# First block of a two-block transformer kernel: queries and keys both scaled on VectorE, squares and scalings placed behind the values, beginning and end reordered

## The chip, the cores and the metric

The kernel runs on one core of a Trainium2 chip. A core has TensorE (PE in the profile; its weight loads are a row of their own, PEld), VectorE (DVE), ScalarE (ACT), GpSimd (POOL) and SyncE (SP), which here only issues DMAs. Each engine works off its own instructions strictly in the order in which they are written; engines wait for one another through semaphores. TensorE writes to PSUM, eight banks of 128 x 512 float32 numbers, and the other engines read the results from there. The metric is the device time of one execution in microseconds (us), lower is better; the median of three runs before the change is 2383.7 us (2383.65 to 2383.8).

## What is computed

All data are float32. The input x is 8 batches of 512 tokens of width 256. Two transformer blocks run one after the other. The change touches only the first; the second is left as it is. The first block, cut to what matters:

```python
mod = silu(c) @ adaln_w.T + adaln_b          # 9 rows of 256: shift, scale, gate for three stages
h = modulate(ln(x), shift_sa, scale_sa)
q = ln(_heads(h, 16)) * qn_w + qn_b          # 16 heads of 16; keys the same with kn_w, kn_b
k = ln(_heads(h, 16)) * kn_w + kn_b
v = _heads(h, 16)
x = x + gate_sa * softmax(q k / 4) v         # self-attention
h = modulate(ln(x), shift_ca, scale_ca)      # cross-attention with 64 context tokens
x = x + gate_ca * (softmax(q' k' / 4) v' @ ca_out_w.T + ca_out_b)
h = modulate(ln(x), shift_ff, scale_ff)
x = x + gate_ff * (silu(h @ w1.T) * (h @ w3.T) @ w2.T)
```

Queries, keys and values of the self-attention have no projection: the normalised heads of one batch are transposed once, and the transposed tile is scaled twice, into q and into k.

## The kernel before

**Stages in a pipeline over batches.** `fast_path` gives each batch three objects: `SelfAttention` (sa), `CrossAttention` (ca) and `FeedForward` (ff). `beginning()` runs the self-attention of batch 0 together with the set-up (modulation, keys and values of the context). Then `cycle(c)` for c = 1 to 7 runs the self-attention of batch c (s), the cross-attention of batch c-1 (x), the feed-forward of batch c-2 (up) and the second half of the feed-forward of batch c-3 (down), and prepares the self-attention of batch c+1 (nxt). In cycle 1 it also makes the second block's keys of the context (`keys1`). `ending()` finishes the last cross-attention and the last two feed-forwards and opens the second block. All of this is under a manual schedule for PE, DVE, ACT and POOL: the order of the calls is the order of the instructions on each of these engines. SP's order is left to the planner.

**Groups.** A batch's self-attention is four groups g = 0 to 3 (s0 to s3 below) of four heads. A group has four key tiles kt. `score(g, kt)` makes four products of 512 columns, one bank each, one for each head (they run side by side in four row strips of TensorE), and `exponentials` turns each into a tile p on ACT. `value(g, kt)` multiplies p with the values, which carry a column of ones for the sum of the softmax; all four kt add into one bank, which ACT copies to `oT` (L565). `back(g)` transposes it, divides and adds to x. `group` (L712) sets the order: the first two scores, then what is `beside`, the other two scores, what is `short`, the values, and the `rest`. In each cycle a further group of two scores and two values, the cross-attention's, stands between s2 and s3 (the "x group" below).

**Queries and keys.** `queries_keys(g)` (L534) transposes four tiles of z into one bank; ACT makes q of it (L543) and DVE makes k (L544). The next group's scores need both. z itself comes from four steps for each half c of the heads: `centre` (DVE, L512 to L514), `square` (ACT, L518), `var` (DVE, L524 and L525) and `scale` (POOL, a power of -1/2 at L531 and a product at L532).

**The ring of banks.** `bank()` and `bank_x()` deal the eight PSUM banks out in turn: the n-th request waits until the reader of request n-8 is done. So the order of the requests decides which reader a matmul waits for.

**The sums of the cross-attention.** `value(c)` of the cross-attention copies the sums to `den` and sends them through DRAM to be laid out anew; `inverse(c)` (L648) takes reciprocals and sends them through DRAM again to be spread over partitions as `rb`, of which there is one buffer; `scaled(c)` (L658, DVE) multiplies `oT` with `rb`. The second `rb` can be loaded only when `scaled(0)` has read the first. `out` (L662) needs both scaled halves.

**The beginning.** The modulation of all batches is a product with `sc32`, which a DVE copy inside `setup` (L740) fills, behind the variance of the second set of heads.

Of the kernel before, what the change touches and what calls it, by code (L numbers as in the profile page):

```python
# [12 lines left out]
AF = mybir.ActivationFunctionType  # L13
# [31 lines left out]
def fast_path(ctx: ExitStack, tc: tile.TileContext, a: dict, out: bass.AP):  # L45
# [237 lines left out]
    nc.vector.scalar_tensor_tensor(scT, scT, 1.0, cT, ALU.add, ALU.mult)  # L283
    nc.vector.tensor_scalar_mul(scT, scT, 0.5)
    nc.vector.tensor_copy(sc0, scT[:, :, 0:1].to_broadcast([P, 2, P]))
    awake(6)
    for k in range(2):
        mm(first_mod, sc0[:, k, :], adaw[:, k, 0 : 2 * D], k == 0, False)
# [168 lines left out]
    class SelfAttention:  # L457
# [76 lines left out]
        def queries_keys(self, g):  # L534

            c, par = divmod(g, 2)
            ps = bank()
            lo = par * HD0
            for t in range(NT):
                nc.tensor.transpose(ps[:, t * P : (t + 1) * P], zs[c][:, t, lo : lo + P], ident)  # L540
            q = wk.tile([P, N], F32, tag="q", name="q", bufs=1)
            k = wk.tile([P, N], F32, tag="k", name="k", bufs=1)
            nc.scalar.activation(q, ps, AF.Identity, bias=qk_cols[:, 1:2], scale=qk_cols[:, 0:1])  # L543
            nc.vector.tensor_scalar(k, ps, col("kw"), col("kb"), ALU.mult, ALU.add)  # L544
            self.s[g] = (q, k)

# [175 lines left out]
    def beginning():  # L722
# [14 lines left out]
        def head_of(s, c, par=None):  # L737
            return [lambda: s.centre(c, par), lambda: s.square(c, par), lambda: s.var(c, par), lambda: s.scale(c, par)]

        def setup():  # L740
            nc.vector.tensor_copy(sc32[:, :, 0:B], scT)
            modulation()

        def bk_columns():
            nc.vector.tensor_scalar(bk_even, col("bk"), col("parity")[:, 0:1], 1.0, ALU.mult, ALU.mult)

        def ones_next():
            nc.gpsimd.memset(hs[1][:, :, :, HD0 + 1 : 32], 0.0)
            nc.gpsimd.memset(hs[1][:, :, :, HD0 : HD0 + 1], 1.0)

        scores, values = of_self(s, 0)
        group(scores, [lambda: s.first_modulated(fm, 0, 1), *head_of(s, 0, 1), setup, lambda: s.first_modulated(fm, 1)],
              [], values, [modulation_columns, lambda: s.queries_keys(1), *head_of(s, 1)])
        scores, values = of_self(s, 1)
        group(scores, [modulation_end, lambda: context0(0), lambda: spread(s.s["gate"], 0, G_SA, D), lambda: context0(1),
                       bk_columns, ones_next],
              [], values, [lambda: s.queries_keys(2), lambda: s.back(0), lambda: nxt.norm(0), lambda: nxt.norm(1)])
        scores, values = of_self(s, 2)
        group(scores, [lambda: keys0(0), lambda: nxt.norm(2), lambda: nc.gpsimd.memset(vb0, 0.0), lambda: keys0(1)],
              [lambda: s.queries_keys(3), lambda: s.back(1), ctx_pieces[0]], values,  # L760
              [lambda: nxt.centre(0), lambda: nxt.square(0), ctx_pieces[1]])
        scores, values = of_self(s, 3)
        group(scores, [lambda: nxt.var(0), lambda: nxt.scale(0), lambda: values0(0), lambda: values0(1), ctx_pieces[2],
                       lambda: nc.vector.tensor_copy(c32[:, :, 0:B], cT)],
              [lambda: s.back(2), lambda: values0(2), lambda: values0(3), modulation1], values,
              [lambda: nxt.centre(1), lambda: context1(0), lambda: context1(1), modulation1_columns,
               lambda: nxt.square(1), lambda: nxt.queries_keys(0), lambda: nxt.var(1), lambda: nxt.scale(1)])

    def cycle(c):

        s, nxt, prev = sa[c], of(sa, c + 1), sa[c - 1]
        x, done = ca[c - 1], of(ca, c - 2)
        up, down = of(ff, c - 2), of(ff, c - 3)
        keys = [lambda p=p: keys1(p) for p in range(NPAIR)] if c == 1 else [lambda: None] * NPAIR
        store = store_keys1 if c == 1 else lambda g: None

        scores, values = of_self(s, 0)
        group(scores, [keys[0], keys[1], lambda: done.out(0), lambda: done.out(1), lambda: up.prepare(0), lambda: up.prepare(1),
                       lambda: down.down(0), lambda: up.prepare(2)],
              [lambda: s.queries_keys(1), lambda: prev.back(3), up.turn, lambda: nxt.norm(0), lambda: nxt.norm(1)], values)  # L780
        scores, values = of_self(s, 1)
        group(scores, [keys[2], lambda: store(0), lambda: down.down(1), lambda: x.prepare(0), lambda: x.prepare(1),
                       lambda: up.up(0), lambda: x.prepare(2), keys[3], lambda: up.up(1)],
              [lambda: s.queries_keys(2), lambda: s.back(0), x.turn, lambda: nxt.norm(2)], values)
        scores, values = of_self(s, 2)
        group(scores, [keys[4], lambda: store(1), lambda: up.up(2), lambda: up.up(3), lambda: x.queries(0), lambda: x.queries(1)],
              [lambda: s.queries_keys(3), lambda: s.back(1), lambda: nxt.centre(0), lambda: nxt.square(0)], values)
        group([lambda: x.score(0), lambda: x.score(1)],
              [keys[5], lambda: up.up(4), keys[6], lambda: up.up(5), lambda: s.back(2), lambda: nxt.var(0), lambda: nxt.scale(0),
               lambda: nxt.centre(1)], [], [lambda: x.value(0), lambda: x.value(1)])  # L790
        scores, values = of_self(s, 3)
        group(scores, [keys[7], lambda: store(2), lambda: up.up(6), lambda: x.inverse(0), lambda: x.inverse(1), lambda: up.up(7),
                       lambda: x.scaled(0)],
              [lambda: nxt.queries_keys(0), lambda: nxt.square(1), lambda: x.scaled(1), lambda: nxt.var(1), lambda: nxt.scale(1)],
              values)
        store(3)

    def ending():

        x, last, up = ca[B - 1], ff[B - 1], ff[B - 2]  # L800
        for fn in (lambda: ca[B - 2].out(0), lambda: ca[B - 2].out(1), lambda: sa[B - 1].back(3), lambda: up.prepare(0),
                   lambda: up.prepare(1), lambda: ff[B - 3].down(0), lambda: up.prepare(2), lambda: x.prepare(0),
                   lambda: x.prepare(1), up.turn, lambda: ff[B - 3].down(1), lambda: x.prepare(2), lambda: up.up(0),
                   x.turn, lambda: up.up(1), lambda: up.up(2), lambda: x.queries(0), lambda: x.queries(1), lambda: up.up(3)):
            fn()
        group([lambda: x.score(0), lambda: x.score(1)], [lambda: up.up(4), lambda: up.up(5)], [],
              [lambda: x.value(0), lambda: x.value(1)])
        for fn in (lambda: up.up(6), lambda: x.inverse(0), lambda: x.inverse(1), open_block1, lambda: up.up(7),
                   lambda: x.scaled(0), lambda: first_norm(0), lambda: first_norm(1), lambda: up.down(0), lambda: x.scaled(1),
                   lambda: x.out(0), lambda: x.out(1), lambda: last.prepare(0), lambda: last.prepare(1),  # L810
                   lambda: up.down(1), lambda: last.prepare(2), lambda: first_norm(2), first_turn, last.turn):
            fn()
        for f in range(8):
            last.up(f)
# [1474 lines left out]
```

## Time and profile before

| | us |
|---|---|
| runs, median of 3 | 2383.7 |
| the profiled execution | 2381.86 |
| its span, first to last instruction | 2379.9 |
| first block with its loads, until `last.up` starts | 842.8 |
| of it: until the first scores of cycle 1 | 96.1 |
| cycles 1, 2, 3, 4, 5, 6, 7 | 74.4, 92.2, 96.2, 97.9, 99.5, 96.2, 94.2 |
| `ending()` until `last.up` | 96.3 |
| from there to the end (last feed-forward, second block) | 1537.1 |

The profile is of one execution, which took 2381.86 us, 1.8 us less than the median of the runs; 2.0 us of it lie outside the span. The page lists busy time for each engine, the granted clock of TensorE in tenths of full speed (PEclk), the chain of work that ended last, and groups of instructions with the idle time before them. In timelines, each row has the start, the time until the last of its instructions ended, the engine, the line of the kernel, what is written and read, the shape, the number of instructions, and in brackets how long the engine sat idle and what released it. A float32 matmul shows as two instructions, so one score of four heads and one kt is x8.

### The profile page before, as it was taken

Reading aid. Unit: us, or ns where it says so; the run is one execution under the profiler, and the core shown is the slowest. Engines: PE = TensorE matmul, PEld = TensorE weight load, DVE = VectorE, ACT = ScalarE, POOL = GpSimd, SP = SyncE. Lnnn points to the kernel's source line nnn. Section 1 sums busy time; section 2 is a strip of 40 time slices with the busy share of each in tenths; the row PEclk is TensorE's granted clock in tenths of the full one; section 3 lists DMA queues with packets and bytes.
Section 4 is the critical chain, followed back from the end, with each engine's and each line's share of the span. In section 5 each row is a group of like instructions: output and inputs, shape, how many; then the busy total and the mean of one; then the engine's idle time right before and its main releaser. Section 6 shows DMA issues by size and latency. Waiting matters only on the chain.

```text
span 2379.9 us, 31143 instructions
## 1 busy us (share of the span) xinstructions
PE 2321.5 (98%) x12372; PEld 1183.2 (50%) x12372; DVE 990.6 (42%) x1879; ACT 883.8 (37%) x1341; POOL 919.5 (39%) x581
## 2 busy tenths in 40 slices
PE   8999999999999899999999999999999999999998
PEld 4434535445355453344434443434354566567666
DVE  3544544444433334434443444444434555432110
ACT  3565455545553213433333334342423221221221
POOL 3553333223221005545455545454544544432110
PEclk8889999999999999999999999999999999999999
DMA  5121000000000300000010001000014222211000
GB/s 186 37 72 37 18 12 16 14 10 18 11 3 12 96 0 10 20 20 19 19 24 15 27 12 28 10 28 11 28 41 122 64 65 74 75 59 37 18 23 19
DMA packets 83738, 83.98 MB, mean 35 GB/s; under 512 B 42128, under 2 KB 59264, under 8 KB 83584
## 3 DMA queue, kind: packets, MB, share of 16 engines
q1 hardware_dynamic: 82104, 78.73, 11.3%
q8 instruction: 100, 1.64, 0.3%
q0 software_dynamic: 576, 2.10, 0.2%
q10 hardware_dynamic: 904, 1.07, 0.2%
q14 instruction: 54, 0.44, 0.1%
HBM read 71.83 MB, written 10.04 MB: 34 GB/s over the span
## 4 chain that ended last, share of the span: by engine, by line
PE 89%; ACT 3%; DVE 3%; DMA 2%; issue 1%; POOL 0%; SPq 0%; ACTq 0%; DVEq 0%; POOLq 0%
PE ps_P L88 40%; PE ps_B L88 26%; PE ps_X L88 7%; PE ps_S L88 6%; PE ps_D L88 5%; PE ps_O L88 4%; ACT p L589 2%; DMA rb<-rec 1%; DVE k L544 1%; PE ps_B L401 1%; ACT q L543 1%; DMA den<-den 0%; PE ps_B L572 0%; PE ps_B L540 0%; DVE z L514 0%
## 5 line engine op out<-in xcount | busy, mean ns | idle before, releaser
L589 ACT ACTIVATE p<-ps_B 128x512 f32<-128x512 f32 x576 | 291.7, 623 | 172.2 <-PE ps_B L88 172.1
L1028 ACT ACTIVATE p<-ps_P 128x1024 f32<-128x1024 f32 x256 | 244.9, 1026 | 95.4 <-PE ps_P L88 95.4
L88 PE MATMUL ps_P<-q,k 32*128 32x512 f32 x2048 | 238.9, 600 | 0.5 <-DVE t L1007 0.5
L88 PE MATMUL ps_B<-hT,w 128*128 128x512 f32 x512 | 235.1, 614 | 0.0
L1037 POOL TENSOR_TENSOR sm<-sm,p 128x1024 f32<-128x1024 f32 x64 | 174.9, 2733 | 139.5 <-ACT p L1028 139.4
L88 PE MATMUL ps_P<-p,v 128*32 128x512 f32 x2048 | 226.4, 594 | 0.0
L996 ACT COPY v<-ps_P 128x1024 f32<-128x1024 f32 x32 | 32.4, 1012 | 375.6 <-PE ps_P L88 375.6
L154 POOL TENSOR_TENSOR rstd<-rstd,mhalf 128x4 f32<-128x4 f32 x49 | 52.0, 1061 | 298.7 <-DVE rstd L153 297.3
L88 PEld LDWEIGHTS ps_P<-q,k 32*128 32x128 f32 x2048 | 100.0, 184 | 133.3 <-issue 105.6
L88 PEld LDWEIGHTS ps_B<-hT,w 128*128 128x128 f32 x512 | 98.4, 196 | 131.3 <-issue 106.1
L1037 DVE TENSOR_TENSOR sm<-sm,p 128x1024 f32<-128x1024 f32 x64 | 98.3, 1537 | 150.6 <-ACT p L1028 150.6
L88 PE MATMUL ps_B<-q,k 16*128 16x512 f32 x1024 | 144.6, 629 | 11.1 <-DVE k L544 9.3
L88 PEld LDWEIGHTS ps_P<-p,v 128*32 128x32 f32 x2048 | 63.3, 110 | 158.3 <-issue 134.8
L1035 POOL TENSOR_TENSOR sm<-p 128x1024 f32<-128x1024 f32 x32 | 79.1, 2471 | 160.8 <-ACT p L1028 160.8
L583 POOL TENSOR_TENSOR attn<-attn,gate 128x256 f32<-128x256 f32 x32 | 23.3, 728 | 303.1 <-DVE attn L581 302.0
L531 POOL TENSOR_TENSOR var<-var,mhalf 128x32 f32<-128x32 f32 (+1 forms) x17 | 87.5, 5149 | 112.7 <-DVE var L525 66.7
L1006 DVE TENSOR_TENSOR t<-ps_P,rope_c 128x1024 f32<-128x1024 f32 x64 | 78.4, 1224 | 106.3 <-POOL q L1010 65.9
L88 PE MATMUL ps_B<-p,h 128*32 128x512 f32 x1024 | 120.4, 604 | 0.0
L88 PE MATMUL ps_P<-hT,w_sa_wq 128*128 128x512 f32 x256 | 118.3, 605 | 0.0
L88 PE MATMUL ps_B<-w,hid 128*128 128x256 f32 x512 | 115.4, 384 | 2.5 <-DVE hid L697 2.5
L1035 DVE TENSOR_TENSOR sm<-p 128x1024 f32<-128x1024 f32 x32 | 39.2, 1225 | 185.9 <-ACT p L1028 185.9
L88 PE MATMUL ps_P<-hT,w_sa_wk 128*128 128x512 f32 x256 | 115.1, 592 | 0.0
(257 smaller groups left out, 3684.4 us busy)
## 6 DMA issues: line engine op xcount, KB each, us to landing
rb<-rec SPq DMA_DIRECT2D x128, 128.0 KB
rb<-rec_d SPq DMA_DIRECT2D x124, 128.0 KB
rb<-rec SPq DMA_DIRECT2D x16, 256.0 KB
out_dram<-x SPq DMA_DIRECT2D x15, 256.0 KB
x<-in_x_dram SPq DMA_DIRECT2D x7, 512.0 KB
gate<-modd SPq DMA_DIRECT2D x24, 128.0 KB
k_d<-q POOLq DMA_DIRECT2D x4, 512.0 KB, 3.4
v_d<-v SPq DMA_DIRECT2D x4, 512.0 KB
```

Source lines behind the costliest of these rows:

```text
L88: nc.tensor.matmul(o, lhsT, rhs, start=start, stop=stop)
L154: nc.gpsimd.tensor_tensor(r[:, :n], r[:, :n], mhalf[:, :n], ALU.pow)
L401: nc.tensor.transpose(ps[:, t * P : (t + 1) * P], z[:, t, k * P : (k + 1) * P], ident)
L531: nc.gpsimd.tensor_tensor(var, var, half, ALU.pow)
L543: nc.scalar.activation(q, ps, AF.Identity, bias=qk_cols[:, 1:2], scale=qk_cols[:, 0:1])
L544: nc.vector.tensor_scalar(k, ps, col("kw"), col("kb"), ALU.mult, ALU.add)
L589: nc.scalar.activation(p[i], ps, AF.Exp, scale=HD0 ** -0.5)
L996: nc.scalar.copy(s["v", half][:, t0 : t0 + 2, :], ps)
L1006: nc.vector.tensor_tensor(c, ps, rope_c[:, None, :].to_broadcast([P, 2, N]), ALU.mult)
L1028: nc.scalar.activation(pr, pss[u], AF.Exp, scale=HD1 ** -0.5)
L1035: eng.tensor_tensor(s["sm", g, u], s["p", g, 0, u], s["p", g, 1, u], ALU.add)
L1037: eng.tensor_tensor(s["sm", g, u], s["sm", g, u], s["p", g, kt, u], ALU.add)
```

## The change

- `sc32` is filled right after `scT` is made (L286), no longer inside `setup`.
- q is made by DVE as k is, from the same bank, with scale and bias as two operands (L543).
- `beginning()`: in group 0 the modulation stands between the square and the variance of the second set of heads; the other half of the heads, `queries_keys(1)`, the modulation's columns, its end and `context0(0)` follow the values. From group 1 on `queries_keys(g+1)` and `back(g-1)` stand ahead of the values. Keys and values of the context, the context's norm and the second block's modulation are dealt out anew; the first square of the next batch moves from group 2 to the front of group 3, its `centre(1)` and `queries_keys(0)` ahead of group 3's values.
- `cycle(c)`: the next batch's `square(0)` moves from the short part of s2, ahead of the values' copy on ACT, into the x group behind its scores; `square(1)` moves from the short part of s3 to beside it; `x.scaled(0)` and `x.scaled(1)` move back, the first to the end of the short part of s3, the second behind s3's values. In cycle 2 alone, `up.turn` moves from s0's short part to beside s1.
- `ending()`: `down(0)` and the preparation of the last cross-attention come first, `out` of the cross-attention before it later, `up.up` of six of its eight parts later relative to the scores, the last feed-forward's preparation ahead of `up.down(0)`, and `last.turn` ahead of `first_turn`.

```diff
+    nc.vector.tensor_copy(sc32[:, :, 0:B], scT)
...
-            nc.scalar.activation(q, ps, AF.Identity, bias=qk_cols[:, 1:2], scale=qk_cols[:, 0:1])
+            nc.vector.tensor_scalar(q, ps, qk_cols[:, 0:1], qk_cols[:, 1:2], ALU.mult, ALU.add)
...
         scores, values = of_self(s, 0)
-        group(scores, [lambda: s.first_modulated(fm, 0, 1), *head_of(s, 0, 1), setup, lambda: s.first_modulated(fm, 1)],
-              [], values, [modulation_columns, lambda: s.queries_keys(1), *head_of(s, 1)])
+        group(scores, [lambda: s.first_modulated(fm, 0, 1), *head_of(s, 0, 1)[:2], modulation, *head_of(s, 0, 1)[2:]],
+              [], values, [lambda: s.first_modulated(fm, 1), *head_of(s, 1)[:2], lambda: s.queries_keys(1), *head_of(s, 1)[2:],
+                           modulation_columns, modulation_end, lambda: context0(0)])
         scores, values = of_self(s, 1)
-        group(scores, [modulation_end, lambda: context0(0), lambda: spread(s.s["gate"], 0, G_SA, D), lambda: context0(1),
-                       bk_columns, ones_next],
-              [], values, [lambda: s.queries_keys(2), lambda: s.back(0), lambda: nxt.norm(0), lambda: nxt.norm(1)])
+        group(scores, [lambda: spread(s.s["gate"], 0, G_SA, D), lambda: context0(1), bk_columns, ones_next],
+              [lambda: s.queries_keys(2), lambda: s.back(0), lambda: nxt.norm(0), lambda: nxt.norm(1)], values,
+              [lambda: keys0(0)])
         scores, values = of_self(s, 2)
-        group(scores, [lambda: keys0(0), lambda: nxt.norm(2), lambda: nc.gpsimd.memset(vb0, 0.0), lambda: keys0(1)],
-              [lambda: s.queries_keys(3), lambda: s.back(1), ctx_pieces[0]], values,
-              [lambda: nxt.centre(0), lambda: nxt.square(0), ctx_pieces[1]])
+        group(scores, [lambda: nxt.norm(2), lambda: nc.gpsimd.memset(vb0, 0.0), lambda: keys0(1), ctx_pieces[0]],
+              [lambda: s.queries_keys(3), lambda: s.back(1), lambda: nxt.centre(0)], values,
+              [lambda: values0(0), lambda: values0(1)])
         scores, values = of_self(s, 3)
-        group(scores, [lambda: nxt.var(0), lambda: nxt.scale(0), lambda: values0(0), lambda: values0(1), ctx_pieces[2],
-                       lambda: nc.vector.tensor_copy(c32[:, :, 0:B], cT)],
-              [lambda: s.back(2), lambda: values0(2), lambda: values0(3), modulation1], values,
-              [lambda: nxt.centre(1), lambda: context1(0), lambda: context1(1), modulation1_columns,
-               lambda: nxt.square(1), lambda: nxt.queries_keys(0), lambda: nxt.var(1), lambda: nxt.scale(1)])
+        group(scores, [lambda: nxt.square(0), lambda: nxt.var(0), lambda: nxt.scale(0), lambda: values0(2), ctx_pieces[1],
+                       ctx_pieces[2], lambda: nc.vector.tensor_copy(c32[:, :, 0:B], cT)],
+              [lambda: s.back(2), lambda: values0(3), lambda: nxt.centre(1), lambda: nxt.queries_keys(0)],
+              [modulation1, *values],
+              [lambda: context1(0), lambda: nxt.square(1), lambda: context1(1), modulation1_columns,
+               lambda: nxt.var(1), lambda: nxt.scale(1)])
...
+        early, late = ([], [up.turn]) if c == 2 else ([up.turn], [])
...
-              [lambda: s.queries_keys(3), lambda: s.back(1), lambda: nxt.centre(0), lambda: nxt.square(0)], values)
+              [lambda: s.queries_keys(3), lambda: s.back(1), lambda: nxt.centre(0)], values)
         group([lambda: x.score(0), lambda: x.score(1)],
-              [keys[5], lambda: up.up(4), keys[6], lambda: up.up(5), lambda: s.back(2), lambda: nxt.var(0), lambda: nxt.scale(0),
-               lambda: nxt.centre(1)], [], [lambda: x.value(0), lambda: x.value(1)])
+              [keys[5], lambda: nxt.square(0), lambda: up.up(4), keys[6], lambda: up.up(5), lambda: s.back(2), lambda: nxt.var(0),
+               lambda: nxt.scale(0), lambda: nxt.centre(1)], [], [lambda: x.value(0), lambda: x.value(1)])
         scores, values = of_self(s, 3)
-        group(scores, [keys[7], lambda: store(2), lambda: up.up(6), lambda: x.inverse(0), lambda: x.inverse(1), lambda: up.up(7),
-                       lambda: x.scaled(0)],
-              [lambda: nxt.queries_keys(0), lambda: nxt.square(1), lambda: x.scaled(1), lambda: nxt.var(1), lambda: nxt.scale(1)],
-              values)
+        group(scores, [keys[7], lambda: store(2), lambda: up.up(6), lambda: x.inverse(0), lambda: x.inverse(1), lambda: nxt.square(1),
+                       lambda: up.up(7)],
+              [lambda: nxt.queries_keys(0), lambda: nxt.var(1), lambda: nxt.scale(1), lambda: x.scaled(0)],
+              values, [lambda: x.scaled(1)])
```

The new order of `ending()` (its three lists are written anew):

```python
for fn in (lambda: sa[B - 1].back(3), lambda: ff[B - 3].down(0), lambda: x.prepare(0), lambda: x.prepare(1),
           lambda: ca[B - 2].out(0), lambda: x.prepare(2), lambda: ca[B - 2].out(1), lambda: up.prepare(0),
           lambda: up.prepare(1), lambda: ff[B - 3].down(1), lambda: up.prepare(2), x.turn, up.turn,
           lambda: x.queries(0), lambda: x.queries(1), lambda: up.up(0), lambda: up.up(1)):
    fn()
group([lambda: x.score(0), lambda: x.score(1)], [lambda: up.up(2), lambda: up.up(3)], [],
      [lambda: x.value(0), lambda: x.value(1)])
for fn in (lambda: up.up(4), lambda: x.inverse(0), lambda: x.inverse(1), open_block1, lambda: up.up(5), lambda: up.up(6),
           lambda: x.scaled(0), lambda: up.up(7), lambda: x.scaled(1), lambda: x.out(0), lambda: x.out(1),
           lambda: last.prepare(0), lambda: last.prepare(1), lambda: up.down(0), lambda: last.prepare(2),
           lambda: first_norm(0), lambda: first_norm(1), lambda: up.down(1), lambda: first_norm(2), last.turn, first_turn):
    fn()
```

## The prediction

> **What bounds the kernel now.** I read the page first, then the run in stages, then TensorE's own timeline in the stages that show gaps.
>
> ```profile
> PE 2321.5 (98%) x12372; PEld 1183.2 (50%) x12372; DVE 990.6 (42%) x1879; ACT 883.8 (37%) x1341; POOL 919.5 (39%) x581
> ...
> PEclk8889999999999999999999999999999999999999
> ```
>
> TensorE is busy nearly all the time and no other engine is half busy, so time is gained only where TensorE idles or runs at a lower granted clock. Both occur early: the clock row is at 8 in the first slices.
>
> ```profile
> 19.94:40.91 20.97, 14.90 (x89) 4.55 (x88) 5.20 (x16) 9.81 (x19) 3.52 (x2) 0.76 0.81 276
> 40.91:60.45 19.54, 17.02 (x84) 6.34 (x84) 5.47 (x12) 9.82 (x19) 7.46 (x4) 0.83 0.01 2
> ...
> 262.59:358.77 96.18, 93.34 (x505) 46.88 (x505) 44.62 (x119) 51.47 (x99) 29.65 (x19) 1.00 0.06 14
> 358.77:456.65 97.88, 95.04 (x505) 47.47 (x505) 42.92 (x107) 51.56 (x99) 29.60 (x19) 0.98 0.05 14
> ...
> 746.46:842.79 96.33, 82.99 (x316) 52.71 (x317) 40.34 (x100) 16.84 (x28) 8.56 (x8) 0.94 0.20 61
> ```
>
> These are stages: length, then busy time of PE, PEld, DVE, ACT, POOL, then the clock. The second block, 1537 us after 842.79, is full and untouched. The first block has its holes in the beginning (19.94 to 96.06), in the ending (746.46 to 842.79), and once in each cycle. The beginning's first hole:
>
> ```profile
> 19.94 2.00 PE L88 MATMUL ps_B<-q,k 16*128 16x512 f32 x16
> 26.30 3.64 PE L88 MATMUL ps_B<-adaw,sc 128*32 128x512 f32 x16 [4.36 <-DVE sc L741]
> 29.87 3.80 PE L88 MATMUL ps_B<-q,k 16*128 16x512 f32 x16
> ```
>
> TensorE waits 4.36 us for a DVE copy of 0.17 us (L741) that stands behind a variance, and then runs at half rate: 3.80 us for scores that took 2.00. The hole of a cycle, in cycle 4 and, below it, the same place in cycle 7, where there is no next batch:
>
> ```profile
> 421.53 2.26 PE L88 MATMUL ps_B<-q,kb 32*128 32x512 f32 x14
> 425.95 1.12 PE L88 MATMUL ps_B<-q,kb 32*128 32x512 f32 x2 [2.16 <-ACT oT L565]
> 427.01 5.40 PE L88 MATMUL ps_B<-hT,w 128*128 128x512 f32 x8
> ```
>
> ```profile
> 715.09 2.19 PE L88 MATMUL ps_B<-q,kb 32*128 32x512 f32 x16
> 717.21 4.99 PE L88 MATMUL ps_B<-hT,w 128*128 128x512 f32 x11
> ```
>
> The eighth score needs the bank of `oT`; ACT copies it only after a square (L518, at 424.80) that waits for DVE's `centre`. Cycle 7 has no such square: there the feed-forward starts 2.12 us after the first score, in cycle 4 5.48 us after.
>
> **The beginning.** Worked through group by group with before's durations. The weights of the modulation are there: SP's next use of that load's semaphore was released by 13.85.
> - Group 0 (scores at 19.94). The modulation follows at 21.94, 16 matmuls in column strips, 1.72 us instead of 3.64. Scores 2 and 3 follow the exponentials out of the banks until 26. ACT: eight exponentials to 25.1, a square to 25.4, eight more (4.03) to 29.45; values end 30.4. Behind them transposes, modulation end and `context0(0)` fill TensorE until 34.1, while DVE makes q and k (0.8 each) by 32.5. Next scores 34.1, before 40.91.
> - Group 1: exponentials 35.3 to 43.3, values end 44, `keys0(0)` 1.7; next scores 45.7, before 60.45. The chain transposes, q on ACT, k on DVE stood behind the values there (57.16 to 60.45) and now lies beside the exponentials; context products at half rate (5.52 for eight) become 3.4.
> - Group 2: eight exponentials from 46.9, the copy of `keys0(1)`, eight more to 55.7, values 56.5, `values0` twice 1.7; next scores 58.2, before 75.34.
> - Group 3 loses some back. ACT reaches `square(0)` after eight exponentials at 63.4; var to 65.0; POOL power 5.4 and product 1.1 to 71.5. Now TensorE's transposes for cycle 1 stand ahead of group 3's values and wait for that; POOL's power for the context's norm (1.0) stands behind too, so DVE's context rows (1.3) and `c32` come at 74.1, and `modulation1` (1.1), values (3.5) and context transposes (1.3) end at 80.0. TensorE idles some 8 of 11 us here, so I add 2.4 for half rate: first scores of cycle 1 at 82.4, before 96.06. **13.7 us less**, bounds 9 (half rate also in group 2, and a longer group 3) and 17.
>
> **q on DVE.** DVE waited 118.8 us in all for ACT's q before k (29 of 32 waits). DVE takes 0.81 for k, so q is bounded by 0.81 (k's row) and 0.78 (ACT's row). [...] q and k are now ready 1.7 us after the transposes, beside 3.6 us of values; without that cover they would cost 1.6 a group. TensorE's waits for k before scores go: two of 0.28 in cycles 1 and 3 to 7, one in cycle 2: 13 x 0.28, **3.6 us less**. The wait of 0.62 at the start of cycles 3 to 7 is counted below.
>
> **The square behind the scores.** 5.48 minus 2.12 is 3.36; group times (306.28 to 343.92 against 696.01 to 730.36) give 3.29. Cycles 1 to 6: **19.8 us less**. The square then delays only the tanh of `up(4)`, whose banks are free of need for 3 us; POOL still has `scale(0)` ready some 6 us before its transposes.
>
> **The scalings behind the values give back.** In cycle 4, with X = 436.20, the start of the cross-attention's values:
>
> ```profile
> 453.12 0.69 DVE L660 TENSOR_TENSOR oT<-oT,rb 128x512 f32<-128x512 f32 x1 [2.41 <-DMA rb<-rec]
> 455.78 0.81 DVE L544 TENSOR_SCALAR k<-ps_B,cols 128x512 f32<-128x512 f32 x1 [1.97 <-ACT q L543]
> 457.63 0.69 DVE L660 TENSOR_TENSOR oT<-oT,rb 128x512 f32<-128x512 f32 x1 [1.04 <-DMA rb<-rec]
> ```
>
> `rb` has one buffer: the second load starts when `scaled(0)` is done (453.81) and lands 3.8 us later. After the change q, k and the variance stand ahead of `scaled(0)`: it starts at X+18.55 instead of X+16.9, `scaled(1)` ends at X+23.8 instead of X+22.1. TensorE, without its 0.62 wait, reaches the second half of `out(0)` at X+22.3: a stall of 1.5. `out` ends at X+27.1 instead of X+26.1, so **1.0 us more** at five passages (cycles 2 to 6), 5.0. Bounds: 0 (load lands faster) and 2 each. From cycle 1 to 2 the round trip through DRAM bounds already (`out` at 174.33), so the 1.6 us that k waited there bring nothing. Leaving cycle 7, `out` comes 7 us later and is covered. What SP has queued behind the waiting load are gates of the next cycle, needed 6 us on.
>
> **The clock.** After the hole of the x group the feed-forward ran at half rate in cycles 1, 2, 4, 5: 8.83 for sixteen in cycle 4 against 7.13 in cycle 7, 1.7; 1.7 for cycles 1 and 2; cycle 5 is 3.3 longer than cycle 3. Together 8.4. [...] By the row all 8.4 go; as cycle 7 also fell to half rate later, at 732, I take 70%, 5.9, and charge the five new stalls a third of 1.7 each, 2.8: **3.1 less**, bounds -4 and +8.
>
> **Cycle 2's `up.turn`.** Before it waited 2.3 us for z at 184.97; now its hT stands on ACT behind eight exponentials (4.03), ahead of `up(0)`: a stall of 3.1 for a saved 2.3 and its half rate. **0**, bounds ±2.
>
> **The ending**, from 746.46. Down, `out` twice and down again (17.3) cover the preparations; `up.turn` waits some 2 us for z, which shares one buffer with `x.turn`. The scores come at 779, the values at 788 instead of 798.17, but behind them stand 13.8 us of `up` where 13.9 stood before, while the second `rb` needs 24.9 from the start of the values (823.02 minus 798.17): `out` stalls 8.4 in one piece, before 2.6+0.5+4.4. Gained is the 3.3 us wait for z at 838.77 and 2.0 at 760.88, for a new 2 at `first_turn`. `last.up` starts 88.3 after, plus 4 for half rate: 92.3 instead of 96.33. **4.0 less**, bounds 0 and 8.
>
> **Sum.** 13.7 + 3.6 + 19.8 - 5.0 + 3.1 + 0 + 4.0 = 39.2. The profiled execution, 2381.86, becomes 2342.7; the runs lie 1.8 above it: 2344.
>
> **Rivals.**
> - The cycles give most back: each new `out` stall brings half rate (1.7 each) and the x group's half rate stays. Then 5.9 are not saved and the half rate costs 8.5 instead of 2.8, 11.6 in all: 2356. For it: cycle 7's fall at 732 without a hole of 2 us. Against: cycles 3 and 6 kept clock 1.00.
> - The beginning gives 5 and the ending nothing, because POOL's chain in group 3 and the DRAM trip bound: 2344+8.7+4 = 2357. For it: POOL's 5.4 us powers; against: groups 0 to 2 hold 17 us of serial waits.
> - No new stall at `out` and no half rate: 5.0+2.8+2.5 better: 2334.
> - Slower: the stall at `out` takes TensorE to half rate and holds it. Its place is the start of cycles 3 to 7; after the long wait at 172 fourteen `out` matmuls took 5.53 (sixteen took 3.72 at 458.58), about 2 us lost, the worst row there is. It decides from 9 us a passage (39.2/5 + 1.0), some 16 us of half rate at each; at 10 us the time is 2389. No row comes near it.
> - The change does not do what it says: the four engines keep the written order, only SP's DMAs are placed by the planner; `rb` or weight loads placed worse in the ending cost a few us, within the bounds.
>
> **Chances.** Forecast 0.60 (its own range 2335 to 2353), cycles giving back 0.14, beginning and ending weak 0.10, better 0.11, slower 0.05. The range 2331 to 2361 takes in all but the slower case and tails. A difference under 0.2% (4.8 us) can't be told from none: faster 0.93, same 0.02, slower 0.05.
>
> **What would show it.** Group 0's modulation matmul should start near 22 with no wait on `sc`; cycle 1's first scores near 82; in the x group no wait on `oT` and 2.1 us from first score to feed-forward; no DVE wait of k on ACT; a new wait of `out` on L660 of about 1.5 in cycles 3 to 7 and of 8 in the ending. Wrong: cycle times still 96 to 99, or `out` stalls over 5 us.

## The result, and the profile after

The kernel after the change takes 2347.12 us in the median of 4 runs (2343.39 to 2350.16); the kernel before took 2383.75 in the same comparison. The ratio is 0.9844 (95% interval 0.9824 to 0.9863). The profiled execution took 2344.22 us, its span is 2342.4.

The page of the kernel after, engine totals and clock row:

```profile
PE 2299.6 (98%) x12372; PEld 1174.4 (50%) x12372; DVE 1016.1 (43%) x1911; ACT 863.8 (37%) x1309; POOL 921.5 (39%) x581
...
PEclk9999999999999999999999999999999999999999
```

32 instructions have gone over from ACT to DVE, and the 8s at the start of the clock row have gone. The same kernel by stages (length, busy time of PE, PEld, DVE, ACT, POOL, clock, DMA share, GB/s):

```profile
19.70:34.05 14.35, 14.35 (x98) 5.25 (x97) 8.47 (x22) 9.36 (x19) 4.70 (x3) 1.00 1.07 361
...
238.84:333.60 94.76, 93.55 (x506) 46.78 (x505) 48.12 (x123) 49.29 (x94) 30.03 (x20) 0.98 0.05 14
333.60:428.84 95.24, 93.61 (x505) 46.79 (x505) 45.73 (x111) 49.29 (x94) 29.97 (x20) 0.98 0.05 14
...
709.96:803.96 94.00, 82.07 (x316) 52.66 (x317) 42.19 (x100) 16.24 (x28) 8.65 (x8) 0.93 0.21 63
```

Group 0 of the beginning is full: 14.35 us of 14.35, where before it was 14.90 of 20.97. Cycle 3, once 96.18, takes 94.76, and cycle 4, once 97.88, takes 95.24. But both granted clocks are now 0.98; cycle 3 had 1.00 before. The places that were holes, in TensorE's timeline of the kernel after:

```profile
21.63 1.92 PE L88 MATMUL ps_B<-adaw,sc 128*32 128x512 f32 x16
...
397.79 2.00 PE L88 MATMUL ps_B<-q,kb 32*128 32x512 f32 x16
399.72 7.13 PE L88 MATMUL ps_B<-hT,w 128*128 128x512 f32 x16
```

The modulation's matmul starts at 21.63 with no bracket behind it, so it waits for nothing. In the x group the feed-forward starts 1.93 us after the first score, where it took 5.48, and runs at full rate. What is new is a wait at the start of a cycle, here in all engines' timeline, cycle 5 (its first scores are at 428.84):

```profile
427.50 0.68 DVE L661 TENSOR_TENSOR oT<-oT,rb 128x512 f32<-128x512 f32 x1
...
430.77 0.70 PE L88 MATMUL ps_B<-w_o,oT 128*128 128x256 f32 x2
431.92 0.69 DVE L661 TENSOR_TENSOR oT<-oT,rb 128x512 f32<-128x512 f32 x1 [3.74 <-DMA rb<-rec]
432.67 3.29 PE L88 MATMUL ps_B<-w_o,oT 128*128 128x256 f32 x14 [1.20 <-DVE oT L661]
```

`scaled(0)` is done at 428.18, the second `rb` lands 3.74 us later, and TensorE, which has the first two matmuls of `out` behind it, idles for 1.20 us. In the ending of the kernel after it is the same wait, larger:

```profile
775.06 0.70 PE L88 MATMUL ps_B<-w_o,oT 128*128 128x256 f32 x2 [3.73 <-DVE oT L661]
780.46 6.28 PE L88 MATMUL ps_B<-w_o,oT 128*128 128x256 f32 x14 [4.70 <-DVE oT L661]
```

The two waits sum to 8.43 us, and the fourteen matmuls behind them take 6.28 against 3.29 above, at half rate (the clock record of this trace has half rate from 776.3 to 786.5).

Where the time went, stage by stage. `both` and `again` are runs described below: two parts of the change alone, and the kernel after a second time, on one chip. `best_d` is the fastest variant. Each column is one profiled execution.

| us | before | after | both | again | best_d |
|---|---|---|---|---|---|
| until the first scores of cycle 1 | 96.06 | 84.06 | 92.57 | 83.92 | 81.22 |
| cycles 1 and 2 | 166.53 | 154.78 | 154.85 | 154.70 | 154.50 |
| cycles 3 to 6 | 389.72 | 377.92 | 366.80 | 377.67 | 368.17 |
| cycle 7 | 94.14 | 93.20 | 93.40 | 93.10 | 91.76 |
| ending, until `last.up` | 96.34 | 94.00 | 95.39 | 92.35 | 86.51 |
| the rest, untouched | 1537.13 | 1538.47 | 1538.76 | 1536.69 | 1538.61 |
| end | 2379.92 | 2342.43 | 2341.77 | 2338.43 | 2320.77 |

Of the 37.5 us between before and after, 12.0 come from the beginning, 11.75 from cycles 1 and 2, 12.7 from cycles 3 to 7 and 2.3 from the ending; the untouched rest took 1.3 more.

### The profile page after: what moved, and what is told of

Read it like the earlier page. It is cut to its first block, busy times and chain, and to the rows that moved or that the text cites. A ratio compares the mean times of both kernels' runs of the same rounds, so it can differ in the third digit from the quotient of the medians.

```text
span 2342.4 us, 31156 instructions
## 1 busy us (share of the span) xinstructions
PE 2299.6 (98%) x12372; PEld 1174.4 (50%) x12372; DVE 1016.1 (43%) x1911; ACT 863.8 (37%) x1309; POOL 921.5 (39%) x581
## 4 chain that ended last, share of the span: by engine, by line
PE 93%; DVE 3%; DMA 2%; POOL 1%; ACT 1%; issue 1%; SPq 0%; ACTq 0%; POOLq 0%; DVEq 0%
PE ps_P L88 40%; PE ps_B L88 28%; PE ps_X L88 7%; PE ps_S L88 6%; PE ps_D L88 5%; PE ps_O L88 4%; DMA rb<-rec 2%; PE ps_B L541 1%; PE ps_B L402 1%; DMA den<-den 1%; PE ps_B L573 1%; DVE oT L661 0%; POOL var L532 0%; PE ps_X L402 0%; ACT p L590 0%
## 5 line engine op out<-in xcount | busy, mean ns | idle before, releaser
L584 POOL TENSOR_TENSOR attn<-attn,gate 128x256 f32<-128x256 f32 x32 | 23.5, 734 | 240.0 <-DVE attn L582 239.0
L88 PE MATMUL ps_P<-w_sa_wv,hT 128*128 128x512 f32 x256 | 114.9, 592 | 0.0
```

Source lines behind the costliest of these rows:

```text
L88: nc.tensor.matmul(o, lhsT, rhs, start=start, stop=stop)
L584: nc.gpsimd.tensor_tensor(attn, attn, gate.to_broadcast([P, NT, 4, HD0]), ALU.mult)
```

## Experiments

Each ratio is to the kernel before on the same chip. The runs were made on three chips, on which the kernel before had medians of 2382.5, 2384.5 and 2385.0, so a difference in us between runs of different chips carries up to 2.5 us of that.

| run | what it is | median us (range) | ratio, 95% interval |
|---|---|---|---|
| `before_q` | before, q on DVE | 2352.7 (2349.39 to 2354.68) | 0.9861 (0.9846 to 0.9877) |
| `before_square` | before, `square(0)` moved | 2356.75 (2354.71 to 2363.61) | 0.989 (0.9872 to 0.9908) |
| `before_both` | before with these two | 2346.03 (2343.56 to 2350.15) | 0.9842 (0.9828 to 0.9856) |
| `after_again` | after | 2343.57 (2340.23 to 2345.66) | 0.9829 (0.9816 to 0.9843) |
| `q_on_act` | after, q back on ACT | 2367.96 (2366.01 to 2373.77) | 0.9942 (0.992 to 0.9965) |
| `square_back` | after, `square(0)` back | 2353.19 (2340.59 to 2356.66) | 0.9856 (0.9824 to 0.9887) |
| `scaled_early` | after, scalings forward again | 2332.77 (2329.08 to 2339.46) | 0.9794 (0.9772 to 0.9816) |
| `rb_two` | after, two `rb` buffers | 2335.57 (2327.47 to 2336.66) | 0.9799 (0.9782 to 0.9816) |
| `old_beginning` | after with before's `beginning()` | 2346.13 (2345.69 to 2349.84) | 0.9844 (0.9829 to 0.9859) |
| `old_ending` | after with before's `ending()` | 2348.03 (2346.87 to 2349.04) | 0.9845 (0.983 to 0.986) |
| `best_b` | `rb_two` and two more edits | 2326.4 (2323.43 to 2332.59) | 0.9759 (0.9744 to 0.9774) |
| `best_d` | `best_b`, `up.turn` early | 2321.33 (2314.98 to 2326.53) | 0.9728 (0.9707 to 0.9748) |

**Undoing one part: q.** The first question was whether the cycles' gain hangs on the square alone, as the prediction had it.

```diff
-            nc.vector.tensor_scalar(q, ps, qk_cols[:, 0:1], qk_cols[:, 1:2], ALU.mult, ALU.add)
+            nc.scalar.activation(q, ps, AF.Identity, bias=qk_cols[:, 1:2], scale=qk_cols[:, 0:1])
```

> The changed kernel with q made by ACT again (L544), all else as changed. Theory (k's wait on ACT's q is what the move to DVE took away; hidden work otherwise): scores of the next group wait 0.28 again in most groups of cycles 1 to 7, and in the beginning q stands on ACT behind eight exponentials, so that group 1's and 3's scores come 1 to 2 us later: 4 to 7 us more than the changed kernel's 2347.1, so 2351 to 2354. Rival (the order alone made the gain, q's engine is hidden): no change, 2347, with DVE's waits for ACT's q back but no wait of TensorE.

It took 20.8 us more than the kernel after, so both expectations missed, the rival's by most. Its timeline at the start of cycle 5, all engines:

```profile
436.49 0.81 DVE L545 TENSOR_SCALAR k<-ps_B,cols 128x512 f32<-128x512 f32 x1 [5.07 <-ACT q L544]
...
437.35 2.00 PE L88 MATMUL ps_B<-q,k 16*128 16x512 f32 x16 [0.45 <-DVE k L545]
...
442.55 0.69 DVE L661 TENSOR_TENSOR oT<-oT,rb 128x512 f32<-128x512 f32 x1 [3.85 <-DMA rb<-rec]
443.30 2.93 PE L88 MATMUL ps_B<-w_o,oT 128*128 128x256 f32 x6 [3.32 <-DVE oT L661]
```

With q on ACT, k is late, `scaled(0)` behind it too, and the second `rb` lands after a cycle's start by 5.2 us instead of 3.1: `out` waits 3.32 us instead of 1.20. Cycles 3 to 6 take 99.0 to 99.7 us. Together they are 19.4 us longer than in the kernel after: 7.6 of it are waits of `out` and 1.8 waits for k, and up to 8.5 is half rate, of which they have 27.3 us instead of 10.2.

**Undoing one part: the square.**

```diff
-              [lambda: s.queries_keys(3), lambda: s.back(1), lambda: nxt.centre(0)], values)
+              [lambda: s.queries_keys(3), lambda: s.back(1), lambda: nxt.centre(0), lambda: nxt.square(0)], values)
...
-              [keys[5], lambda: nxt.square(0), lambda: up.up(4), keys[6], lambda: up.up(5), lambda: s.back(2), lambda: nxt.var(0),
+              [keys[5], lambda: up.up(4), keys[6], lambda: up.up(5), lambda: s.back(2), lambda: nxt.var(0),
```

> The changed kernel with the next batch's first square back in the short part of s2, in the cycles alone. Theory: the hole of 2.2 us in the cross-attention's scores comes back in cycles 1 to 6, 3.3 us each, 19.8, and half rate after some of them, 3 to 8: 2370 to 2375. Rival (with q off ACT the square is reached and done earlier, so the hole is not whole): 1 to 2 us a cycle, 2353 to 2359.

The median is 6.1 us above the kernel after; the two intervals overlap, but the rival's 2353 is met and the theory's 2370 is not. The hole did not come back: in the trace the sixteen scores of the x group take 3.07 us instead of 2.00, a hole of 1.1 and not of 3.4. So what made the hole was not the square alone.

**One part alone, each way, and both.** Three kernels start from the kernel before: `before_q` has the reverse of the first diff above, `before_square` the reverse of the second, `before_both` the two together.

> The kernel before with one edit: q made by DVE (L543), order unchanged. Theory now (the hole in the cross-attention's scores hung on a chain: exponentials, q on ACT, k, back and centre on DVE, square and copy on ACT; q on DVE cuts it at its first link): the hole shrinks from 2.2 us of wait to a slow eighth score, some 2.3 us less in each of cycles 1 to 6, plus 0.3 to 0.6 at the group starts and part of the half rate: 18 to 28 us less than before. Rival (the prediction's own account: the hole hangs on the square's place, q on DVE brings 3.6): 3 to 5 us less.

> The kernel before with one edit: the next batch's first square from the short part of s2 to behind the cross-attention's scores; q still on ACT. Theory now (moving the square cuts the same chain at its last link; either edit is enough): 3.3 us less in each of cycles 1 to 6 and part of the half rate after it, 20 to 26 us less than before, the same gain as q on DVE alone, so the two do not add. Rival (with q on ACT the copy of oT comes late anyway): under 8 us.

> The kernel before with two parts of the change together: q on VectorE, and the next batch's square(0) behind the scores of the cross-attention group. Theory (both parts cut the same chain exponentials -> q -> k -> back -> centre -> square -> copy of oT, so the second brings nearly nothing): about as the better of the two alone, 2346 to 2354, cycles 3 to 6 at 92 to 94.5 us. Rival A (two separate holes that add, as the prediction took it): 32 + 28 less, 2322 to 2328, cycles at 88 to 90. Rival B (each removes its own half rate): 2334 to 2342.

Each alone brings most of the gain (31.8 and 27.8 us against the before of their own chip); together they bring 39.0, not the 59.6 of their sum, as theory said. Each alone brings somewhat more than theory gave it (18 to 28 and 20 to 26), and the second is not quite worth nothing, as theory had it for `before_both`: it adds 7.2 or 11.2. The cycle explains it. This is the chain in the kernel before, cycle 4, all engines:

```profile
416.13 4.03 ACT L589 ACTIVATE p<-ps_B 128x512 f32<-128x512 f32 x8 [5.60 <-PE ps_B L88]
...
420.01 0.80 ACT L543 ACTIVATE q<-ps_B,qk_cols 128x512 f32<-128x512 f32 x1
420.84 0.81 DVE L544 TENSOR_SCALAR k<-ps_B,cols 128x512 f32<-128x512 f32 x1 [5.01 <-ACT q L543]
...
423.55 1.16 DVE L514 TENSOR_TENSOR z<-h,mean 128x512 f32<-128x512 f32 x1
...
424.80 0.63 ACT L518 ACTIVATE ln<-z 128x512 f32<-128x512 f32 x1 [3.99 <-DVE z L514]
425.33 0.57 ACT L565 COPY oT<-ps_B 128x512 f32<-128x512 f32 x1
```

Each line waits for the one above: q for eight exponentials on ACT, k for q, the centre behind k (with `back` between), the square for the centre, the copy of `oT` behind the square. TensorE waits at the end of it. The same stretch in `before_q`:

```profile
401.44 4.03 ACT L589 ACTIVATE p<-ps_B 128x512 f32<-128x512 f32 x8 [5.60 <-PE ps_B L88]
...
403.68 0.80 DVE L544 TENSOR_SCALAR k<-ps_B,cols 128x512 f32<-128x512 f32 x1
...
406.85 3.07 PE L88 MATMUL ps_B<-q,kb 32*128 32x512 f32 x16
407.64 0.63 ACT L518 ACTIVATE ln<-z 128x512 f32<-128x512 f32 x1 [2.17 <-DVE z L514]
408.17 0.57 ACT L565 COPY oT<-ps_B 128x512 f32<-128x512 f32 x1
```

k starts 2.24 us after the exponentials instead of 4.71, and the copy of `oT` 6.73 instead of 9.20: all 2.5 us are handed down the chain. About 1 us of hole is left. In `before_square`, q and k are as late as ever, but the copy no longer stands behind them:

```profile
411.90 2.19 PE L88 MATMUL ps_B<-q,kb 32*128 32x512 f32 x16
...
412.12 0.59 ACT L565 COPY oT<-ps_B 128x512 f32<-128x512 f32 x1 [0.94 <-PE ps_B L88]
```

Here ACT idles 0.94 us and is ready when TensorE's values are. Cycle 3 closes the account, as its clock was 1.00 in before and after each edit but one: 96.18 in before, 92.68 with q, 94.55 with the square (with 3.4 us of half rate; cycle 4, without it, 92.85), 91.62 with both. The square alone saves 3.3 and q alone 3.5, both together 4.56, so 2.3 are the same microseconds. What q adds on top of the square, 1.2, is as much as the scores' waits for k that the prediction counts in a cycle (0.28 twice and 0.62).

**The rest of the change against these two parts.**

> The kernel after once more, to stand beside before_both on the same chip: the theory that beginning, ending and scalings of the change together bring little over its two parts q and square expects the same time as before_both within 5 us, 2344 to 2350; the prediction's sum (beginning 13.7 and ending 4.0 less, scalings 5.0 more) expects it 13 us faster than before_both.

The whole change is 2.5 us ahead of `before_both`, and the intervals overlap: what everything but the two edits brings can't be told from nothing. So theory's 5 us hold and the prediction's 13 do not. In the table of stages (both against again) the new beginning is 8.65 us ahead at cycle 1 and keeps it through cycle 2, the ending gains 3.0, and cycles 3 to 6 give back 10.9, of which 5.1 is half rate (10.2 us of it against none). Cycle 4 of `before_both` by windows, with the start of its cycle 5 (all engines):

```profile
339.04:430.70 91.66, 91.63 (x506) 46.18 (x505) 46.50 (x111) 49.18 (x94) 29.59 (x19) 1.00 0.05 14
```

```profile
427.87 0.69 DVE L660 TENSOR_TENSOR oT<-oT,rb 128x512 f32<-128x512 f32 x1 [2.59 <-DMA rb<-rec]
...
432.53 0.69 DVE L660 TENSOR_TENSOR oT<-oT,rb 128x512 f32<-128x512 f32 x1 [2.52 <-DMA rb<-rec]
432.63 3.94 PE L88 MATMUL ps_B<-w_o,oT 128*128 128x256 f32 x16
```

With q on DVE and the scalings in their old place, TensorE is busy for 91.63 of 91.66 us: no idle time is left there. `scaled(0)` stands before q and k, and `scaled(1)` comes in time: the sixteen matmuls of `out` run without a wait.

**The scalings.** Two edits take the new wait away from the kernel after. `scaled_early` puts `scaled(0)` before q and k and `scaled(1)` right behind them; `rb_two` keeps the order and gives `rb` a second buffer (space from a work tile cut from 64 to 8 columns and from one gate buffer less).

```diff
-                       lambda: up.up(7)],
-              [lambda: nxt.queries_keys(0), lambda: nxt.var(1), lambda: nxt.scale(1), lambda: x.scaled(0)],
-              values, [lambda: x.scaled(1)])
+                       lambda: up.up(7), lambda: x.scaled(0)],
+              [lambda: nxt.queries_keys(0), lambda: x.scaled(1), lambda: nxt.var(1), lambda: nxt.scale(1)],
+              values)
```

> The changed kernel with x.scaled(0) ahead of q and k of the next batch again, and x.scaled(1) right behind them, as before the change. Theory (the second load of rb, which waits for scaled(0), makes out wait): the five stalls of 1.3 to 1.6 us at out in cycles 3 to 7 go, q and k lie still beside the values: 7 us less, 2340. Rival (DVE stands in order behind the load of rb, so q and k come late instead): the next cycle's scores wait 0.5 to 1.5 and the time stays at 2345 to 2348.

```diff
-            s["rb", c] = rb = wk2.tile([P, N], F32, tag="rb", name="rb", bufs=1)
+            s["rb", c] = rb = wk2.tile([P, N], F32, tag="rb", name="rb", bufs=2)
```

> The changed kernel with two buffers for rb (the space for it from a smaller rstd tile and one gate buffer less). Theory (one buffer ties the second load to the first multiplication): the stalls of out go in cycles 3 to 7, 7 us, and of the ending's 8.8 us of stall at out the second part, 4.9, mostly goes: 2336 to 2338. Rival (the load itself takes the time, the two loads share the DMA engines and the weights' traffic in the ending): stalls shrink by half only, 2342 to 2344. In the passage from cycle 1 to 2, 3.7 us of stall should shrink too.

Both win, 14.4 and 11.6 us against the kernel after (10.8 and 8.0 against `after_again`), and cycles 3 to 6 go to 91.6 to 91.9 (`scaled_early`) and 91.6 to 93.3 (`rb_two`). This is cycle 4 of `rb_two`:

```profile
328.17:420.02 91.85, 91.67 (x506) 46.27 (x505) 45.65 (x112) 49.19 (x94) 30.58 (x20) 1.00 0.05 15
```

In cycles 3 to 6 of `rb_two` TensorE has no wait for a scaled half, where the kernel after has four, 5.0 us together. The order is the same, so the single `rb` is the cause of the new wait. `scaled_early` beat its expectation by 7. Its trace has no half rate in cycles 3 to 6, where the kernel after has 10.2 us of it, a loss of 5.1; by the last section this hangs on where the cycles fall on a grid in time, and not on the wait by itself.

**Beginning and ending.** Each was replaced by that of before, all else as after.

```diff
-             [lambda: s.first_modulated(fm, 0, 1), *head_of(s, 0, 1)[:2], modulation, *head_of(s, 0, 1)[2:]],
+             [lambda: s.first_modulated(fm, 0, 1), *head_of(s, 0, 1), setup, lambda: s.first_modulated(fm, 1)],
...
```

> The changed kernel with the beginning of before (its sc32 copy inside it), q on DVE. Theory (the new order of the beginning is worth what its stage lost, 12 us, and keeps TensorE's clock up in cycle 1, 3.3 us): 2347 + 12 to 15 = 2359 to 2362, less by up to 4 where q on DVE alone helps the old order's groups. Rival (in the old order, too, q on DVE makes most of the gain): 2350 to 2353. First scores of cycle 1 at 93 to 96 by the first, at 86 to 89 by the second.

```diff
-        for fn in (lambda: sa[B - 1].back(3), lambda: ff[B - 3].down(0), lambda: x.prepare(0), lambda: x.prepare(1),
+        for fn in (lambda: ca[B - 2].out(0), lambda: ca[B - 2].out(1), lambda: sa[B - 1].back(3), lambda: up.prepare(0),
...
```

> After with the ending() of before. Theory (the stall of out for the scaled halves lasts to the DRAM trip either way): the ending as in the runs of before's order with q on VectorE, 96 to 99.5 us instead of 94.0, so 2349 to 2353. Rival (the new order of the ending only shifts the stall): 2345 to 2348.

`old_beginning` had its first scores of cycle 1 at 92.28, 8.2 us later than the kernel after, and yet was no slower (2346.13 against 2347.12 and 2343.57); both expectations missed. At cycle 3 it was 6.2 us behind (245.01 against 238.84). The rest went with things that this edit does not touch: 1.9 us in cycles 3 to 7 (half rate in two of them instead of three), and 3.1 in the untouched second block, which took 1535.39 in that run. How much of the beginning's 8 us reaches the end stays open; by the medians it is between -1 and 2.6. `old_ending` needs 98.42 us to `last.up`, where the new order takes 94.00 and 92.35, and is 4.5 us slower than `after_again` on the same chip, as large as the 4.0 that the prediction put on it, though the intervals of the two ratios overlap; its time lies between what theory and rival named.

**Combined.** `best_b` is `rb_two` with two edits: in group 3 the context's transposes come first and `queries_keys(0)` moves behind the values (so that no matmul of group 3 stands behind POOL's power), and in the ending `up.down(0)` comes ahead of `out`. `best_d` also puts cycle 2's `up.turn` back where it stood.

```diff
-        group(scores, [lambda: nxt.square(0), lambda: nxt.var(0), lambda: nxt.scale(0), lambda: values0(2), ctx_pieces[1],
+        group(scores, [ctx_pieces[1], lambda: nxt.square(0), lambda: nxt.var(0), lambda: nxt.scale(0), lambda: values0(2),
...
-                   lambda: x.scaled(0), lambda: up.up(7), lambda: x.scaled(1), lambda: x.out(0), lambda: x.out(1),
-                   lambda: last.prepare(0), lambda: last.prepare(1), lambda: up.down(0), lambda: last.prepare(2),
+                   lambda: x.scaled(0), lambda: up.up(7), lambda: up.down(0), lambda: x.scaled(1), lambda: x.out(0), lambda: x.out(1),
+                   lambda: last.prepare(0), lambda: last.prepare(1), lambda: last.prepare(2),
...
-        early, late = ([], [up.turn]) if c == 2 else ([up.turn], [])
+        early, late = [up.turn], []
```

> A version meant to beat both: two buffers for rb; in the beginning's last group the context's norm ahead of the power on POOL and queries_keys(0) behind the values; in the ending down(0) ahead of out. Theory: against rb_two (2327 to 2336), the wait of 3.8 us for POOL and the 1.3 for c32 go, the stage shrinks by 4 to 6 with its half rate; of the ending's 7.6 us of stall at out some 6 go: 2318 to 2326. Rival (k of cycle 1 comes late behind values and transposes, and the last preparation then bounds the ending): 2328 to 2335.

> The fastest combination so far (after with two rb buffers, the context transposes first in group 3, down(0) ahead of out in the ending) with cycle 2's up.turn back where it stood. Theory (the 3.0 us wait for hT in cycle 2 goes and z is ready by then, as cycle 1 is longer than 65 us): 2323 to 2326, no wait for hT in cycle 2. Rival (the wait for z of before, 2.3 us at this place, is back): 2326 to 2329, same as without this edit.

Both beat the two kernels of this study; `best_b` lies at the slow end of what was expected, `best_d` 1.7 us below it. In `best_d`, `out` waits 1.7 us in the whole kernel, where it waited 18.2 after the change. Cycle 2's 2.9 us wait for hT has gone, but a wait of 2.15 for z is back at the old place (162.67), so the expectation of `best_d` was right on the first and wrong on the second; cycle 2 is 1.1 us shorter than in `best_b` (83.81 against 84.87). The rest of what lies between the two profiled executions is the ending, 86.51 against 92.29, at clock 1.00 in this one: the edit doesn't touch it.

## Why the prediction was right, and where it was not

**The time and the stages.** 2344 was predicted, 2347.1 measured, 2343.6 in the second measurement. By stages: beginning 13.7 less against 12.0; cycles 21.5 less (3.6 + 19.8 - 5.0 + 3.1) against 24.5; ending 4.0 less against 2.3 and, the second time, 4.0; the rest 0 against 1.3 more.

**The beginning.** First scores of groups 1, 2, 3 and of cycle 1 were put at 34.1, 45.7, 58.2 and 82.4, and came at 34.05, 46.91, 61.12 and 84.06. Groups 1 and 2 took 1.3 and 1.7 us longer than counted, group 3 took 1.3 less. In group 3 two errors cancel, which is luck: TensorE idled 5.0 us of its 22.94 and not 8, but ran 10.2 us at half rate (69.8 to 80.0), up to 5.1 us lost where 2.4 was put. And the forecast takes it that what is gained until cycle 1 reaches the end, which `old_beginning` does not bear out.

**q on DVE: the step that failed.** "TensorE's waits for k before scores go: [...] **3.6 us less**" counted only the waits in which TensorE names k. The row of DVE waiting 118.8 us for q was read and then priced at what TensorE shows of it. But k is in front of everything else on DVE. Put in alone it brings 31.8 us, on top of the square 11.2 (39.0 less 27.8), and taken out of the kernel after it costs 20.8, there by way of the waits of `out` and half rate.

**The square.** "Cycles 1 to 6: **19.8 us less**", and 5.9 of half rate, is right for the square alone in the kernel before: 27.8. It's wrong as the square's share of the change: once q is on DVE, the square brings 7.2 (39.0 less 31.8), or 6.1 by `square_back`. The proof offered for it, cycle 7, couldn't tell: that cycle lacks not only the square but also the centre ahead of it, and with them the whole chain. The sum was saved because q and the square were put down once as a whole, at nearly what both bring: 4.5 us a cycle (3.3 + 0.6 + 0.6) against 4.56 measured in cycle 3.

**The scalings.** The stall of 1.5 came, at 1.20 in the cycle shown, and its cause, one `rb`, is shown by `rb_two`. What the move costs by itself is 1.5 a cycle (93.15 at full clock in cycle 5 against 91.6 to 91.9 in `before_both`); net of the 0.6 of waiting for k that went, the prediction's 1.0 was right. Half rate came in three of the four cycles 3 to 6, where the prediction charged each with a third of it. There the two make 10.9 us (four times 1.5 and three times 1.7, the excess of 8.83 over 7.13, are 11.1), where the prediction's own terms give 8.7 (four times 1.0, 0.6 and 0.57).

**The clock.** 3.1 net can't be checked by itself. The prediction charged each new stall with a third of 1.7 us of half rate. Cycles 3 to 6 had clock 0.98, 0.98, 1.00 and 0.98 with these stalls, and 1.00 four times in `before_both` without them. But the last section shows that a charge for each stall does not say when half rate comes in these cycles: it hangs on where they fall on a grid in time.

**Cycle 2 and the ending.** hT's stall was put at 3.1 and was 2.9. `out` in the ending was put at 8.4 "in one piece" and is 8.43 in two.

**The rivals.** None came true. "No new stall at `out` and no half rate" named 2334; it's what `scaled_early` (2332.8) and `rb_two` (2335.6) measure, when the stall is taken away.

## What to carry to other kernels

An instruction's price on an engine that works in order is not the wait that the bounding engine shows for its result, but the delay it hands to everything behind it: follow the queue to the next instruction that the bounding engine does wait for. Where several edits cut one chain, their gains don't add; price the chain once, and use as a control a place that lacks one link, not all of them. When a wait goes at one place, ask which buffer with one copy sets the next one: here a second `rb` was worth 8.0 to 11.6 us.

## What the runs showed of the hardware that was not expected

Half rate does not follow the wait that seems to cause it. In the kernel after it came for 3.4 us at 318.9, 414.5 and 602.2, some 80 us after the start of cycles 3, 4 and 6, whose stall of `out` lies some 4 us behind their start; in the 30 us ahead of it TensorE has no wait over 0.3 us. `rb_two` (313.5), `before_square` (333.8) and `best_d` (497.6) have it at the same place in a cycle without that stall. What stands there are the sixteen scores behind the cross-attention's values. They take 3.1 to 3.3 us, where the sixteen at the start of a cycle take 2.00; here in cycles 4 and 5 of the kernel after, and below them the stretch of 3.41 us that tells the two apart, with clock 0.50 in cycle 4 and 1.00 in cycle 5:

```profile
410.79 3.15 PE L88 MATMUL ps_B<-q,k 16*128 16x512 f32 x16
...
505.58 3.20 PE L88 MATMUL ps_B<-q,k 16*128 16x512 f32 x16
```

```profile
414.50:417.91 3.41, 3.41 (x6) 1.35 (x5) 0.18 (x1) 3.00 (x7) 2.06 (x2) 0.50 0.04 6
510.07:513.48 3.41, 3.41 (x9) 1.52 (x8) 1.32 (x3) 2.46 (x5) 1.32 (x2) 1.00 0.03 5
```

The clock records of all fourteen traces tell when it comes. In each trace the stretches at half rate begin on one grid of 3.413 us, which keeps its beat through the whole trace: all 17 in the kernel before, the last 689 steps behind the first, and all 10 in the kernel after, 665 steps (318.9, 414.5 and 602.2 lie 28 and 55 steps apart). In cycle 4 a step begins at 411.08, 0.29 us behind the first of these scores, and the next step is at half rate. In cycle 5 it begins at 506.66, 1.08 us behind, and the clock stays at 1.00, though this cycle has the stall of `out` too. So it is in all 98 cycles (1 to 7 of fourteen traces): half rate follows in the 30 in which a step begins between 0.43 us ahead of the first of these scores and 0.33 behind it, so that it covers at least 2.8 us of them, and in none of the other 68. In the kernels before and after these are four of 14 cycles (cycle 7 before; cycles 3, 4 and 6 after), with a step from 0.04 us ahead to 0.29 behind; in the other ten the next step comes 0.85 to 1.96 us behind the first score. No run made these scores faster, so that this would end the half rate is not shown. At the stall itself it came six times in cycles 3 to 6: four times in `q_on_act`, with waits of 3.0 to 3.3 us, and once each in `old_beginning` (a wait of 1.49) and `old_ending` (1.74), but not at one of 1.73 in `square_back`.

The untouched second block took 1535.4 to 1538.8 us in these executions, with 0.1 to 7.5 us of half rate in it: differences of 3 us between two kernels are of that size.

The centre's subtraction on DVE takes 1.16 us in the kernel before (423.55), where an addition of POOL (L584, 423.43, 0.73 us) runs beside it, and 0.69 us in the kernel after for the second half of the heads (410.39), where this addition (L585) was over by 410.11. In the kernel before the addition ends at 424.16 and the subtraction 0.55 us after that, and all thirteen of the centre's subtractions that meet such an addition in the two kernels take 1.16 to 1.18 us. Beside POOL's power there is no such loss: it runs from 410.06 for 5.44 us in the kernel after, and the subtraction at 410.39 takes its 0.69 us beside it, as do all thirteen that meet a power. What sets the two apart was not shown. The half microsecond (1.16 less 0.69) is part of the chain above; no run here changed it by itself.
